# Taps in two halves, and the last feed-forwards' bias, relu, cast and residual on another engine

## The chip, the cores and the metric

One core of a Trainium2 chip runs the whole program. Its engines each work through their own list of instructions in order and wait for each other by semaphores: TensorE (PE) multiplies matrices into PSUM, VectorE (DVE) and ScalarE (ACT) work element by element on SBUF and PSUM, GpSimd (POOL) element by element on SBUF, and SyncE (SP) issues the transfers. The metric is the device time of one execution, in microseconds (us).

## The reference

Two layers of a small vision network on an input of 2 x 96 x 96 x 96 (batch, channels, rows, columns). Layer 0 adds a state-space block with a selective scan, layer 1 a block of attention over cells of 2 x 2 pixels together with a 5 x 5 depthwise convolution of the values. After either, a feed-forward of 96 - 384 - 96 is added to each pixel's channels:

```python
EXP_MUL, MAN_MUL = (5, 2)
EXP_ACC, MAN_ACC = (5, 10)
q_mul = lambda x: _float_quantize(x, EXP_MUL, MAN_MUL)
q_acc = lambda x: _float_quantize(x, EXP_ACC, MAN_ACC)

def _qlinear(x, W, b):
    y = q_acc(jnp.einsum('bsk,nk->bsn', q_mul(x), q_mul(W)))
    return q_acc(y + q_mul(b))
h = jax.nn.relu(_qlinear(x, W1, b1))
y = _qlinear(h, W2, b2)
...
t = t + _L1_ffn_ref(_ln_t(t), L1_ffn_W1, L1_ffn_b1, L1_ffn_W2, L1_ffn_b2)
```

Products are of 8-bit floats, sums are rounded to 16-bit floats, and so is the sum with the bias. In layer 1 the convolution, and what the feed-forward is given, are

```python
lepe = lax.conv_general_dilated(v.reshape(B, C, H, W), lepe_w, (1, 1), [(pad, pad), (pad, pad)], dimension_numbers=('NCHW', 'OIHW', 'NCHW'), feature_group_count=C)
...
out = out + lepe
out = jnp.einsum('oc,bchw->bohw', proj_w, out) + proj_b[None, :, None, None]
```

## The kernel before

Channels lie on the partitions. Layer 0 goes through 32 stripes (2 batches of 16), each of 6 rows or 576 pixels. For each stripe there is a front, a scan, and a back (`_l0_back`, L936), which projects, runs the feed-forward and stores x2 to device memory at L1015. Layer 1 then takes one batch after the other: `_l1_before` (L1240) loads x2 by stripes (nxt, L1253) and norms and projects them (L1258 to L1273), the attention follows, and at last `_l1_rows` (L1657) goes through 8 strips q = 0 to 7 of R = 12 rows.

A strip of `_l1_rows` projects the values into vch with an edge of two pixels (L1694, L1697), computes the near attention ft (L1719 to L1747), and adds up 21 of the 25 taps of the convolution on VectorE into acc (L1755 to L1765): one multiplication (L1759, 0.9 in the plan) and 20 fused multiply-adds (L1762, 1.43 in the plan), each over all 12 rows, 1152 columns. The other four taps, `ON_PE`, are products on TensorE (L1778). Then `project` (L1767) is called for each half c2 of 6 rows. For each quarter it forms pp on TensorE: four taps from vch (L1778), ft (L1782), and acc (L1788). VectorE adds bias and residual to make x3 (L1791). After both quarters of a half, `_plan_ffn` follows, and the half is stored (L1799).

`_plan_ffn` (L868) works on 576 pixels. The norm goes through TensorE (fxc L879), ScalarE's square (fsq L884), TensorE (fva L890), ScalarE's logarithm and exponential (L862, L863: frs or, in layer 0, in place), and VectorE's product with a cast to 8 bits (fxq L894). The hidden layer has NM = 3 blocks of 128 units. For each, TensorE forms fph (L906) for both quarters, ScalarE casts them to 16 bits (fh16, L909), adds the bias and takes the relu in place (L913), and casts to 8 bits (fh8, L916). TensorE forms fpy from the three blocks (L924), ScalarE casts it (fy16, L927) and adds the bias in place (L931), and GpSimd adds the residual x1 and gives x2 (L932).

The order of work is not that of the code. Each helper only records operations with an engine, a cost and the tiles that they read and write. `_Plan.order` (L153) then plays them through: of the operations whose operands and buffers are ready it takes for each engine the one that can start first, and among equals the one that is due first. The due times come from `_dues` (L848), which spreads the operations of a strip, as they were recorded, over a span of time (for strip q from 40 q to 40 q + 80). The instructions are issued in this order, and `_in_order` (L57) ties each engine to it. So what an engine does next is fixed at build time, and an instruction that waits holds all that stand behind it on its engine. A key beside a tile, such as (h16, m), limits a dependency to that part of the tile.

Buffers of one stage are given to the next, which waits for what last used the memory: the first loads of `_l1_before` follow the last store of the stage before, and GpSimd's memsets between the layers (L1976, L1983, L1916, L1925) and VectorE's copies (L1979, L1981) follow layer 0's last feed-forward.

Of the kernel before, what the change touches and what calls it, by code (L numbers as in the profile page):

```python
# [14 lines left out]
ALU = mybir.AluOpType  # L15
# [12 lines left out]
HW = 96  # L28
NTOK = HW * HW
WIN = 6  # L30
NW = HW // WIN
SEQ = WIN * WIN
T = WIN * HW
# [13 lines left out]
CELLS = HW // 2  # L47
# [61 lines left out]
class _Plan:  # L109
# [19 lines left out]
    def op(self, eng, cost, run, r=(), w=(), due=0.0, tab=None, also=(), scan=False, first=False):  # L129
        o = _Op(eng, cost * self.rate.get(eng, 1.0), run, due, tab)  # L130
        o.scan, o.first = scan, first
        ref = lambda t: t if isinstance(t, tuple) else (t, None)
        meets = lambda a, b: a is None or b is None or a == b
        for t, key in map(ref, r):
            o.deps.update(p for p, q in t.writes if meets(key, q))
        for t, key in map(ref, w):
            o.deps.update(p for p, q in t.writes + t.reads if meets(key, q))
        for t, key in map(ref, r):
            t.reads.append((o, key))
        for t, key in map(ref, w):  # L140
            t.writes.append((o, key))
        o.deps.discard(o)
        for t in [x[0] for x in map(ref, list(r) + list(w))] + list(also):
            if t not in o.tiles:
                o.tiles.append(t)
        for t in o.tiles:
            if not t.users and t.tag != "p":
                t.queue.append(t)
            t.users.append(o)
        self.ops.append(o)  # L150
        return o
# [713 lines left out]
    op("act", H2, run, (), (v,) if out is None else (v, out), tab="e", times=2)  # L865


def _plan_ffn(k, S, op, ps, temp, pool, bufs, ffn, x1, roomy=False):  # L868


    nc = k.nc
    cols = lambda c: slice(c * H2, (c + 1) * H2)
    xc = None if roomy else temp("fxc")
    s1, xq = temp("fsq"), S.tile(pool, [C, T], "fxq", bufs, F8)
    for c in range(2):
        def norm(c=c):
            pc, va = ps("fxc"), ps("fva")
            rs = S.tile(pool, [C, H2], "frs", 4) if roomy else None
            op("pe", H2, lambda: nc.tensor.matmul(  # L879
                pc.ap[:C, :H2], k.less_mean, x1.ap[:, cols(c)], start=True, stop=True),  # L880
                (x1,), (pc,), () if roomy else (xc,))

            def centred():
                nc.scalar.activation(s1.ap[:, cols(c)], pc.ap[:C, :H2], AF.Square)  # L884
                if not roomy:
                    nc.scalar.copy(xc.ap[:, cols(c)], pc.ap[:C, :H2])

            op("act", H2, centred, (pc,), ((s1, c),) if roomy else ((xc, c), (s1, c)),
               times=1 if roomy else 2)
            op("pe", H2, lambda: nc.tensor.matmul(  # L890
                va.ap[:C, :H2], k.mean96, s1.ap[:, cols(c)], start=True, stop=True),
                ((s1, c),), (va,), (xq,))
            _power(k, op, va, k.eps5, rs)
            op("dve", H2, lambda: nc.vector.tensor_tensor(  # L894
                xq.ap[:, cols(c)], pc.ap[:C, :H2] if roomy else xc.ap[:, cols(c)],
                rs.ap if roomy else va.ap[:C, :H2], ALU.mult, saturate=False),
                (pc, rs) if roomy else ((xc, c), va), ((xq, c),))

        norm()
    h16 = S.tile(pool, [128, NM, T], "fh16", bufs, HP)  # L900
    h8 = S.tile(pool, [128, NM, T], "fh8", bufs, F8)
    for m in range(NM):
        for c in range(2):
            def hidden(m=m, c=c):
                ph = ps("fph")
                op("pe", H2 // 2, lambda: nc.tensor.matmul(  # L906
                    ph.ap[:, :H2], ffn.w1[:, m * 128 : (m + 1) * 128], xq.ap[:, cols(c)],
                    start=True, stop=True), ((xq, c),), (ph,), (h16,))
                op("act", H2, lambda: nc.scalar.copy(h16.ap[:, m, cols(c)], ph.ap[:, :H2]),  # L909
                   (ph,), ((h16, m),))  # L910

            hidden()
        op("act", T, lambda m=m: nc.scalar.activation(  # L913
            h16.ap[:, m, :], h16.ap[:, m, :], AF.Relu, bias=ffn.b1[:, m : m + 1]),
            (), ((h16, m),))
        op("act", T, lambda m=m: nc.scalar.activation(  # L916
            h8.ap[:, m], h16.ap[:, m], AF.Copy, saturate=False), ((h16, m),), ((h8, m),))
    y16, x2 = S.tile(pool, [C, T], "fy16", bufs, HP), temp("x2")
    for c in range(2):
        def last(c=c):  # L920
            py = ps("fpy")

            for m in range(NM):
                op("pe", H2 // 2, lambda m=m: nc.tensor.matmul(  # L924
                    py.ap[:C, :H2], ffn.w2[:, m, :], h8.ap[:, m, cols(c)],
                    start=(m == 0), stop=(m == NM - 1)), (h8,), (py,), (y16,))
            op("act", H2, lambda: nc.scalar.copy(y16.ap[:, cols(c)], py.ap[:C, :H2]),  # L927
               (py,), ((y16, c),))

        last()  # L930
    op("act", T, lambda: nc.scalar.activation(y16.ap, y16.ap, AF.Identity, bias=ffn.b2), (), (y16,))  # L931
    op("pool", T, lambda: nc.gpsimd.tensor_tensor(x2.ap, x1.ap, y16.ap, ALU.add), (x1, y16), (x2,))  # L932
    return x2


def _l0_back(k, P, S, f, ffn, res, dst, at):  # L936

    nc = k.nc
    n0 = len(S.ops)
    Y, zs = f.Y, f.zs  # L940
    temp = lambda name: S.tile(P.back, [C, T], "b", 3, name=name, skip=2)
# [69 lines left out]
    for c in range(2):  # L1011
        project(c)

    x2 = _plan_ffn(k, S, op, ps, temp, P.back, 1, ffn, x1)
    S.op("sp", 1.2, lambda: nc.sync.dma_start(dst, x2.ap), (x2,), ())  # L1015
    _dues(S, n0, at)

# [151 lines left out]
def _layer0(k, tc, a, x, x2d):  # L1169


    nc = k.nc
    with ExitStack() as st:
# [34 lines left out]
        def back(n):  # L1208
            b, s = stripes[n]
            t0, t1 = (64 * n + 68) * tau, (64 * n + 135) * tau  # L1210
            _l0_back(k, P, S, F[n], ffn, x[b, :, s * WIN : (s + 1) * WIN, :],
                     x2d[b, :, s * T : (s + 1) * T], lambda v: t0 + v * (t1 - t0))

        P.wa, P.wb = S.held(k.w_ca, "w_ca"), S.held(k.w_cb, "w_cb")
        c1, split = a["off1"], 128 - C
# [441 lines left out]
def _l1_rows(k, P, S, W, ffn, M, distT, x2, out, q, at):  # L1657
# [94 lines left out]


    acc = S.tile(P.wk, [C, R, HW], "acc", 2)
    for n, t in enumerate(t for t in range(25) if t not in ON_PE):  # L1755
        def tap(n=n, t=t):
            src = lambda: vch.ap[:, t // 5 : t // 5 + R, t % 5 : t % 5 + HW]
            if n == 0:
                S.op("dve", 0.9, lambda: nc.vector.tensor_scalar(  # L1759
                    acc.ap, src(), W.lw[:, t : t + 1], None, ALU.mult), (vch,), (acc,))  # L1760
            else:
                S.op("dve", 1.43, lambda: nc.vector.scalar_tensor_tensor(  # L1762
                    acc.ap, src(), W.lw[:, t : t + 1], acc.ap, ALU.mult, ALU.add), (vch,), (acc,))

        tap()  # L1765

    def project(c2):  # L1767
        xr, x3 = S.tile(P.wk, [C, T], "xr", 2), temp("x3")
        S.op("sp", 1.0, lambda: nc.sync.dma_start(
            xr.ap, x2[:, (2 * q + c2) * T : (2 * q + c2 + 1) * T]), (), (xr,))  # L1770

        def part(c):
            pp = ps("pp")
            r0, cols = c2 * WIN + 3 * c, slice(c * H2, (c + 1) * H2)

            def some():
                for n, t in enumerate(ON_PE):
                    nc.tensor.matmul(  # L1778
                        pp.ap[:C, :H2], W.pt[:, n],
                        vch.ap[:, r0 + t // 5 : r0 + t // 5 + 3, t % 5 : t % 5 + HW],  # L1780
                        start=(n == 0), stop=False)
                nc.tensor.matmul(  # L1782
                    pp.ap[:C, :H2], W.p,
                    ft.ap.rearrange("p i n -> p (i n)")[:, (2 * c2 + c) * H2 : (2 * c2 + c + 1) * H2],
                    start=False, stop=False)

            op("pe", (len(ON_PE) + 1) * H2, some, (vch, ft), (pp,))
            op("pe", H2, lambda: nc.tensor.matmul(  # L1788
                pp.ap[:C, :H2], W.p, acc.ap[:, r0 : r0 + 3, :], start=False, stop=True),
                (acc,), (pp,), (x3,))  # L1790
            op("dve", H2, lambda: nc.vector.scalar_tensor_tensor(  # L1791
                x3.ap[:, cols], pp.ap[:C, :H2], W.pb, xr.ap[:, cols], ALU.add, ALU.add),
                (pp, xr), ((x3, c),))

        for c in range(2):
            part(c)
        y = _plan_ffn(k, S, op, ps, temp, P.wk, 3, ffn, x3, True)
        row = q * R + c2 * WIN
        S.op("sp", 1.0, lambda: nc.sync.dma_start(  # L1799
            out[:, row : row + WIN, :].rearrange("c r w -> c (r w)"), y.ap), (y,), ())  # L1800

    for c2 in range(2):
        project(c2)
    _dues(S, n0, at)

# [241 lines left out]
```

## Time and profile before

| | |
|---|---|
| three runs | 8144.84, 8158.97, 8159.37 us; median 8158.97 |
| profiled execution | 8149.47 us; from first to last instruction 8147.7 us |
| busy | VectorE 7575.8 us (93%), TensorE 7250.8 (89%), ScalarE 6328.2 (78%), GpSimd 5305.7 (65%) |
| mean granted TensorE clock | 0.963 |
| layer 0's last bias, residual, and the first product of layer 1 (start) | 6128.94, 6129.79, 6136.23 us |
| last taps, last residual of batch 0 (start) | 7097.00, 7139.15 us |
| first product of batch 1 in layer 1 (start) | 7146.01 us |
| last taps, last residual of batch 1 (start) | 8101.10, 8143.26 us |

The profile is of one execution. Times are from the first instruction on; a row names the line of the kernel, the engine, the operation and the tiles (output, arrow, inputs), the shape as partitions x columns, and how often. "Idle before" is the time that the engine did nothing ahead of a row, and the arrow names the instruction whose end let it go on. VectorE is the busiest engine over the whole, most of it in layer 0's scans and the attention's sums.

### The profile page before, as it was taken

What the parts mean: (1) busy time and instruction counts of PE and PEld (TensorE: products, weight loads), DVE (VectorE), ACT (ScalarE), POOL (GpSimd) and SP (SyncE); (2) the same over time, 40 slices, a digit from 0 to 9 for tenths busy, and PEclk for the clock granted to TensorE, in tenths of its full rate; (3) what the DMA queues carried; (4) which work ended last, traced back from release to release, by engine and by line L of the source; (5) the groups of instructions that cost most, each with busy time, mean ns of one, the idle gap of its engine ahead of it and who ended that gap; (6) DMA issues with size and microseconds to landing.
All of it is one profiled execution on the core that took longest, in us unless ns stands there. A gap on an engine that the chain in (4) does not pass through costs nothing. (4 is left out here: it accounts for less than half of the span.)

```text
span 8147.7 us, 123836 instructions
## 1 busy us (share of the span) xinstructions
PE 7250.8 (89%) x46031; PEld 3210.3 (39%) x46031; DVE 7575.8 (93%) x5276; ACT 6328.2 (78%) x10672; POOL 5305.7 (65%) x3963
## 2 busy tenths in 40 slices
PE   7888888988888888898888888888878999989998
PEld 3333344444444334343443443343334224532245
DVE  3999999999999999999999999999996998869988
ACT  5788888788788887788887878887747886778867
POOL 4888888888888888888888888888861000110001
PEclk8999999999999999999999999999998999999999
DMA  3545555444545555455445554555431000110001
GB/s 94 165 157 162 159 162 162 154 155 158 163 159 161 160 160 159 155 159 160 153 155 164 160 161 157 161 162 157 154 108 47 3 2 22 32 46 3 3 23 33
DMA packets 359852, 992.23 MB, mean 122 GB/s; under 512 B 69288, under 2 KB 71680, under 8 KB 359040
## 3 DMA queue, kind: packets, MB, share of 16 engines
q1 hardware_dynamic: 357440, 984.04, 38.5%
q8 instruction: 365, 5.98, 0.3%
q14 instruction: 255, 2.09, 0.1%
q10 hardware_dynamic: 1792, 0.12, 0.0%
HBM read 797.19 MB, written 139.25 MB: 115 GB/s over the span
## 5 line engine op out<-in xcount | busy, mean ns | idle before, releaser
L1136 POOL TENSOR_TENSOR h<-h,cre 128x864 f32<-128x864 f32 x2048 | 3481.2, 1714 | 753.5 <-DVE h L1131 507.5
L1131 DVE TENSOR_TENSOR_SCAN h<-dA,bp 128x864 f32<-128x864 f32 x2048 | 3900.0, 1939 | 61.4 <-PE y L1149 39.9
L1094 ACT ACTIVATE dA<-dlr,A 128x576 f32<-128x576 f32 x3072 | 2158.7, 766 | 830.9 <-DVE h L1131 725.4
L1114 DVE TENSOR_TENSOR bp<-dur,bp 128x864 f32<-128x864 f32 x2048 | 2075.4, 1046 | 188.4 <-DMA dur<-du_d 117.3
L1149 PE MATMUL y<-h,fold 128*32 128x288 f32 (+2 forms) x18432 | 1790.0, 434 | 221.7 <-POOL h L1136 198.7
L1509 ACT ACTIVATE pr<-sc 128x960 f32<-128x960 f32 (+1 forms) x1080 | 954.1, 937 | 203.9 <-PE sc L1505 183.4
L1149 PEld LDWEIGHTS y<-h,fold 128*32 128x32 f32 x18432 | 725.9, 113 | 974.9 <-POOL h L1136 669.5
L1110 PE MATMUL bp<-bt,selb 128*128 128x288 bf16 x2048 | 613.5, 300 | 458.7 <-DVE h L1131 440.4
L1589 DVE TENSOR_TENSOR sums<-sums,pr 128x3840 f32<-128x3840 f32 (+1 forms) x240 | 959.1, 3996 | 57.0 <-ACT pr L1509 34.5
L1681 POOL MEMSET vch<- 96x32 f32 x16 | 2.4, 154 | 1321.8 <-DVE dist L1543 1211.3
L1110 PEld LDWEIGHTS <-selb 128*128 128x128 bf16 x2048 | 197.3, 96 | 1163.0 <-DVE h L1131 956.4
L1505 PE MATMUL sc<-qH,kH 32*128 32x480 f32 (+1 forms) x3240 | 627.3, 602 | 12.6 <-issue 8.0
L1505 PE MATMUL sc<-q,kH 32*128 32x480 f32 (+1 forms) x1080 | 564.8, 602 | 0.0
L1194 PE MATMUL y<-selb,minus 128*32 128x288 bf16 x3146 | 552.0, 301 | 0.0
L1571 PE MATMUL av<-pr,vT 128*32 128x480 f32 (+1 forms) x4320 | 534.1, 565 | 3.7 <-ACT av L1596 3.5
L1762 DVE SCALAR_TENSOR_TENSOR acc<-vch,lepe_w,acc 96x1152 f32<-96x1152 f32 x320 | 467.7, 1462 | 8.4 <-ACT vch L1697 0.4
L1505 PEld LDWEIGHTS sc<-qH,kH 32*128 32x128 f32 x3240 | 219.8, 184 | 422.0 <-issue 223.7
L617 PE MATMUL pc<-xin,w_ca 128*128 128x288 f32 x1152 | 366.5, 424 | 0.4 <-DVE fxq L894 0.4
L1194 PEld LDWEIGHTS <-minus 128*32 128x32 bf16 x3146 | 274.0, 100 | 212.5 <-issue 122.3
L932 POOL TENSOR_TENSOR x<-x,fy 96x576 f32<-96x576 f32 x32 | 53.2, 1662 | 461.1 <-ACT fy L931 387.7
L791 PE MATMUL pt<-xd,w_dt 96*128 96x288 f32 x768 | 264.2, 440 | 7.7 <-ACT r L797 4.8
L810 POOL TENSOR_TENSOR e<-e,du 128x576 f32<-128x576 f32 x192 | 231.5, 1206 | 31.0 <-ACT du L806 31.0
(284 smaller groups left out, 10983.1 us busy)
## 6 DMA issues: line engine op xcount, KB each, us to landing
cre<-c_d SPq DMA_DIRECT2D x1024, 288.0 KB, 3.3
dur<-du_d SPq DMA_DIRECT2D x256, 864.0 KB, 5.2
dlr<-dl_d SPq DMA_DIRECT2D x256, 864.0 KB, 5.8
x<-xs SPq DMA_DIRECT2D x512, 72.0 KB, 2.6
du_d<-du SPq DMA_DIRECT2D x128, 288.0 KB, 3.1
dl_d<-dl SPq DMA_DIRECT2D x128, 288.0 KB, 3.7
du_d<-du SPq DMA_DIRECT2D x128, 144.0 KB, 2.5
dl_d<-dl SPq DMA_DIRECT2D x128, 144.0 KB, 2.4
```

The costliest lines, as they stand in the source:

```text
L1094: nc.scalar.activation(dA.ap[:, :, blk, :], dlr.ap[:, blk, :].rearrange("p (c n) -> p c n", c=2), AF.Exp, scale=k.A[:, i, kg, h, blk : blk ...
L1110: nc.tensor.matmul(bp.ap[:, :H2], k.selb[:, kk, i, :], f.bc[o].ap[:, toks], start=True, stop=True)
L1114: nc.vector.tensor_tensor(bp.ap[:, : NBL * H2].rearrange("p (b n) -> p b n", b=NBL)[:, ::-1], dur.ap[:, ::-1, toks], bp.ap[:, :H2].unsquee ...
L1131: nc.vector.tensor_tensor_scan(hv, dv, bv, 0.0, ALU.mult, ALU.add)
L1136: nc.gpsimd.tensor_tensor(ht.ap, ht.ap, cre.ap[:, toks].unsqueeze(1).to_broadcast([128, NBL, H2]), ALU.mult)
L1149: nc.tensor.matmul(dst, k.fold, v, start=start, stop=stop)
L1194: nc.tensor.matmul(P.awake.ap[NBL * CB :, T - HEAD + 2 * 72 : HEAD], k.minus[:, :CB], k.selb[:, 0].rearrange("p i m -> p (i m)")[:, : HEAD ...
L1505: nc.tensor.matmul(two[to // 2][:, to % 2, :n], kH[rows, k0 : k0 + 128], q, start=True, stop=True)
L1509: nc.scalar.activation(pr[:, 2 * i : 2 * i + 2, :n], two[i][:, :, :n], AF.Exp, scale=HD**-0.5)
L1571: nc.tensor.matmul((main if s < HEADS else other)[s * HD : (s + 1) * HD, :n], vT[:, blk, hd, :], pr[:, place(s, p), :n], start=at == 0, st ...
L1589: nc.vector.tensor_tensor(both, both, pr[:, :, :, :n], ALU.add)
L1762: S.op("dve", 1.43, lambda: nc.vector.scalar_tensor_tensor(acc.ap, src(), W.lw[:, t : t + 1], acc.ap, ALU.mult, ALU.add), (vch,), (acc,))
```

## The change

In the last strip of a batch (q = 7) the taps are recorded in two halves of 6 rows, 576 columns each: those of the first half before `project(0)`, those of the second before `project(1)`. Their planned cost is 0.45 for the multiplication and 0.2 + 0.615 for a multiply-add. The product of a half depends on its half of acc alone. Five feed-forwards are "last": both halves of q = 7 in either batch, and that of layer 0's last stripe. In these, bias and relu of the hidden layer, its cast to 8 bits, the output's bias, and the residual are VectorE's; the casts from PSUM stay on ScalarE. Everything else is as before. In the built program TensorE, ScalarE, VectorE and GpSimd differ in order only at these three places, and SyncE not at all.

```diff
-def _plan_ffn(k, S, op, ps, temp, pool, bufs, ffn, x1, roomy=False):
+def _plan_ffn(k, S, op, ps, temp, pool, bufs, ffn, x1, roomy=False, last=False):
...
+        if last:
+            op("dve", T, lambda m=m: nc.vector.tensor_scalar(
+                h16.ap[:, m, :], h16.ap[:, m, :], ffn.b1[:, m : m + 1], 0.0, ALU.add, ALU.max),
+                (), ((h16, m),))
+            op("dve", T, lambda m=m: nc.vector.tensor_copy(
+                h8.ap[:, m], h16.ap[:, m], saturate=False), ((h16, m),), ((h8, m),))
+            continue
         op("act", T, lambda m=m: nc.scalar.activation(
             h16.ap[:, m, :], h16.ap[:, m, :], AF.Relu, bias=ffn.b1[:, m : m + 1]),
             (), ((h16, m),))
...
+    final = last
...
+    if final:
+        op("dve", T, lambda: nc.vector.tensor_scalar(y16.ap, y16.ap, ffn.b2, None, ALU.add), (), (y16,))
+        op("dve", T, lambda: nc.vector.tensor_tensor(x2.ap, x1.ap, y16.ap, ALU.add), (x1, y16), (x2,))
+        return x2
     op("act", T, lambda: nc.scalar.activation(y16.ap, y16.ap, AF.Identity, bias=ffn.b2), (), (y16,))
     op("pool", T, lambda: nc.gpsimd.tensor_tensor(x2.ap, x1.ap, y16.ap, ALU.add), (x1, y16), (x2,))
...
-    for n, t in enumerate(t for t in range(25) if t not in ON_PE):
-        def tap(n=n, t=t):
-            src = lambda: vch.ap[:, t // 5 : t // 5 + R, t % 5 : t % 5 + HW]
...
+    parts = 2 if q == CELLS // WIN - 1 else 1
+    R1 = R // parts
+
+    def tap(n, t, p):
+        src = lambda: vch.ap[:, R1 * p + t // 5 : R1 * p + t // 5 + R1, t % 5 : t % 5 + HW]
+        dst = lambda: acc.ap[:, R1 * p : R1 * p + R1]
+        key = (acc, p) if parts > 1 else acc
+        if n == 0:
+            S.op("dve", 0.9 / parts, lambda: nc.vector.tensor_scalar(
+                dst(), src(), W.lw[:, t : t + 1], None, ALU.mult), (vch,), (key,))
+        else:
+            S.op("dve", 0.2 + 1.23 / parts, lambda: nc.vector.scalar_tensor_tensor(
+                dst(), src(), W.lw[:, t : t + 1], dst(), ALU.mult, ALU.add), (vch,), (key,))
...
-                (acc,), (pp,), (x3,))
+                ((acc, c2) if parts > 1 else acc,), (pp,), (x3,))
...
-        y = _plan_ffn(k, S, op, ps, temp, P.wk, 3, ffn, x3, True)
+        y = _plan_ffn(k, S, op, ps, temp, P.wk, 3, ffn, x3, True, parts > 1)
...
     for c2 in range(2):
+        if c2 < parts:
+            for n, t in enumerate(taps):
+                tap(n, t, c2)
         project(c2)
```

In layer 0 the last stripe's `_l0_back` is called with `last` set (`n == len(stripes) - 1`), and passes it on.

More of the change, by code (lines that the diff above doesn't have):

```diff
@@ L933, in _plan_ffn, with _l0_back @@
     return x2
-def _l0_back(k, P, S, f, ffn, res, dst, at):
+def _l0_back(k, P, S, f, ffn, res, dst, last, at):
     nc = k.nc
@@ L1012, in _l0_back @@
         project(c)
-    x2 = _plan_ffn(k, S, op, ps, temp, P.back, 1, ffn, x1)
+    x2 = _plan_ffn(k, S, op, ps, temp, P.back, 1, ffn, x1, last=last)
     S.op("sp", 1.2, lambda: nc.sync.dma_start(dst, x2.ap), (x2,), ())
@@ L1211, in back @@
             _l0_back(k, P, S, F[n], ffn, x[b, :, s * WIN : (s + 1) * WIN, :],
-                     x2d[b, :, s * T : (s + 1) * T], lambda v: t0 + v * (t1 - t0))
+                     x2d[b, :, s * T : (s + 1) * T], n == len(stripes) - 1, lambda v: t0 + v * (t1 - t0))
         P.wa, P.wb = S.held(k.w_ca, "w_ca"), S.held(k.w_cb, "w_cb")
@@ L1754, in _l1_rows @@
     acc = S.tile(P.wk, [C, R, HW], "acc", 2)
-    for n, t in enumerate(t for t in range(25) if t not in ON_PE):
-        def tap(n=n, t=t):
-            src = lambda: vch.ap[:, t // 5 : t // 5 + R, t % 5 : t % 5 + HW]
[L1758 to L1765, printed above, removed]
+    parts = 2 if q == CELLS // WIN - 1 else 1
[10 more added lines that the diff above has]
+                dst(), src(), W.lw[:, t : t + 1], dst(), ALU.mult, ALU.add), (vch,), (key,))
+    taps = [t for t in range(25) if t not in ON_PE]
     def project(c2):
```

## The prediction

> **What bounds the kernel where it is changed.** The page's busy row (VectorE 93%, ScalarE 78%) is an average over stages; the change touches three short places: the end of layer 0, and the end of layer 1 for batch 0 and for batch 1. So I read the busy table of two stretches of batch 1's end, then the timeline of each engine there. Columns of the table: stretch, length, busy us and instructions of TensorE, weight loads, VectorE, ScalarE, GpSimd, then clock and DMA.
>
> ```profile
> 8073.70:8108.30 34.60, 33.42 (x142) 20.72 (x141) 34.11 (x33) 24.80 (x55) 3.34 (x2) 1.00 0.09 26
> 8108.30:8147.70 39.40, 20.27 (x77) 11.45 (x74) 4.70 (x11) 30.48 (x64) 5.08 (x4) 0.64 0.08 23
> ```
>
> While the last taps run (first row) VectorE is full. Then it is nearly empty for 39.4 us, with ScalarE busy for 30.5. VectorE's and ScalarE's timelines say why (start, duration, instruction, idle time before it and who ended it):
>
> ```profile
> 8101.10 7.21 DVE L1762 SCALAR_TENSOR_TENSOR acc<-vch,lepe_w,acc 96x1152 f32<-96x1152 f32 x5
> 8109.63 0.52 DVE L1791 SCALAR_TENSOR_TENSOR x<-pp,proj_b,xr 96x288 f32<-96x288 f32 x1 [1.32 <-PE pp L1788]
> ...
> 8121.82 0.45 DVE L894 TENSOR_TENSOR fxq<-fxc,frs 96x288 fp8e5<-96x288 f32 x1 [5.90 <-ACT frs L863]
> ...
> 8132.24 0.45 DVE L894 TENSOR_TENSOR fxq<-fxc,frs 96x288 fp8e5<-96x288 f32 x1 [9.16 <-ACT frs L863]
> ```
>
> ```profile
> 8114.55 1.00 ACT L909 CAST fh<-fph 128x288 f16<-128x288 f32 x3 [0.20 <-PE fph L906]
> 8115.59 0.78 ACT L913 ACTIVATE fh<-fh,f1b1g 128x576 f16<-128x576 f16 x1
> 8116.39 0.68 ACT L916 ACTIVATE fh<-fh 128x576 fp8e5<-128x576 f16 x1
> ...
> 8140.03 0.68 ACT L916 ACTIVATE fh<-fh 128x576 fp8e5<-128x576 f16 x1
> ...
> 8142.35 0.77 ACT L931 ACTIVATE fy<-fy,f1b2g 96x576 f16<-96x576 f16 x1
> ```
>
> Three feed-forwards remain after the taps: the second half of q=6 (6b) and both halves of q=7 (7a, 7b); 6a, the first half of q=6, is just being finished. ScalarE takes them in turn without a gap: hidden layers 8114.6 to 8121.0, 8124.8 to 8131.3, 8134.3 to 8140.7. VectorE waits for it 5.9 and 9.2 us. What follows the last bias:
>
> ```profile
> 8143.26 1.27 POOL L932 TENSOR_TENSOR x<-x,fy 96x576 f32<-96x576 f32 x1 [7.46 <-ACT fy L931]
> 7140.45 0.32 SPq L1799 DMA_DIRECT2D out<-x  x1
> 7142.90 5.64 SPq L1253 DMA_DIRECT2D nxt<-x2d  x4
> 7146.01 4.12 PE L1258 MATMUL nxc<-nxt,less_mean 96*96 96x288 f32 x8 [8.22 <-DMA nxt<-x2d]
> ```
>
> The first line ends batch 1: x2 is complete at 8144.53, and the rest to 8147.7 is its store. The others are batch 0's end, the same picture 1004.1 us earlier: the store of x2, then the load of batch 1, then TensorE, idle 8.2 us for it. So what x2 gains is passed on whole. At layer 0's end too: bias until 6129.71, GpSimd's residual until 6131.08, store, load at 6133.38, TensorE at 6136.23 after 7.75 us of idling.
>
> **Prices.** From the list of groups by shape (line, instruction, count, busy us, mean ns):
>
> ```profile
> L1762 DVE SCALAR_TENSOR_TENSOR acc<-vch,lepe_w,acc 96x1152 f32<-96x1152 f32 x320 | 467.7, 1462 | 8.4 <-ACT vch L1697 0.4
> L1759 DVE TENSOR_SCALAR acc<-vch,lepe_w 96x1152 f32<-96x1152 f32 x16 | 13.0, 809 | 16.0 <-DMA xn<-xd 8.2 <-ACT vch L1697 7.8
> L1592 DVE TENSOR_TENSOR sums<-sums 128x960 f32<-128x960 f32 x8 | 9.3, 1158 | 0.3
> L284 DVE CAST f1w1q<-f1w 96x384 fp8e5<-96x384 f32 x1 | 0.4, 356 | 0.6 <-DMA f1b<-in_b 0.6
> L1981 DVE COPY join<-ident 32x32 f32<-32x32 f32 x1 | 4.4, 4447 | 0.0
> ```
>
> - *Half tap.* The adds of 3840 and 3072 columns (4.156 and 3.356 us) give 1.04 ns a column. Five taps in a row take 7.21 us, a step of 1.445; so the fixed part is 1.445 - 1.20 = 0.245, and a half (576 columns) costs 0.845. A rule speaks against halving: the Trainium skill, "VectorE: DVE Perf Modes", section on the TRN2 errata, says that the latency of SBUF is paid per instruction, so many small tiles pay it many times; its formula, N + 151 cycles at 0.96 GHz, is a fixed part of 0.157. By the rule 21 added instructions cost 3.3 us a batch, by the row 5.1. The row counts also the wait of each tap for the one before it, so I take the row.
> - *Fp8 cast* of 576: the cast row and the copies (960 in 0.653, 3840 in 2.155: 0.52 ns a column) give 0.356 + 192 x 0.52 = 0.46.
> - *Bias and relu* on 16-bit data: no row of VectorE has 16-bit input. The nearest is L1759: 0.809 for 1152 fp32 columns, 0.6 plus 0.21 fixed. At that rate 576 cost 0.51. The same page, perf-mode tier table, has tensor_scalar at twice that rate on 16-bit data: an estimate of 0.15 + 0.21 = 0.36. I take 0.36; with 0.51 the final sum is 3 us smaller; at one column per 1.04 ns it would be 0.81.
> - *Residual* (two SBUF inputs, 576): 1.158 - 384 x 1.04 ns = 0.76, against 1.27 on GpSimd.
>
> **Layer 0's end.** ScalarE's six casts stay; the first three end at 6121.87 as before, the rest by 6122.8. Relu and cast of one block of 128 on VectorE are 0.36 + 0.46 = 0.82 with the step between; three blocks from 6121.93 end at 6124.4, where ScalarE ended at 6127.30. From there to the second y16 cast was 1.61 us (6127.30 to 6128.91); it stays: 6126.0. Bias 0.06 + 0.36, residual 0.03 + 0.76: 6127.2 instead of 6131.08. **Gain 3.9 us.** GpSimd's memsets of 4.7 us, queued behind the removed residual, now start after VectorE's bias, beside VectorE's residual. The rule against this ("SBUF — State Buffer", who interferes with whom: a VectorE instruction in a two-port mode, or with two SBUF inputs against a GpSimd reader, waits for the whole GpSimd instruction) is borne out by L1981: 4.447 us for 32 columns, until the memsets ended. Memsets do not read, so I charge the residual nothing; blocked, it would end 4.6 later and the gain would be -0.7. The copies behind it wait, but have until the first xn at about 6139.
>
> **A batch's end (twice).** Times are batch 1's.
> 1. *Taps.* Before: 34.6 us from 8073.69 to 8108.3. Added: 21 x 0.245 = 5.1, and the two adds of x3 for 7a (0.43 each), which now come before the last seven half taps. End 8108.3 + 5.1 + 0.9, less 0.1 for some changes of instruction and stretches by GpSimd: 8114.1. Queued behind them on VectorE: fxq of 6b. Its rs is ready at 8111.5 (8111.4 before; the fpy of 6a starts 0.2 later on TensorE), so it is 2.6 us late; this is what halving costs.
> 2. *What halving buys.* In TensorE's new order the last products of 7a (L1788 in the old numbers) stand before the fpy of 6a. They need the first half's taps: 8073.69 + 0.61 + 20 x 0.845, and 2.6 for the other VectorE instructions among them, is 8093.8. TensorE reaches them at 8102.0, behind the products that fill it, and waits for nothing. x3 of 7a is done at 8107.2 (8111.0 before), and its norm goes ahead of 6b's hidden layer.
> 3. *6b* stays on ScalarE: fxq 8114.1 to 8114.55, first cast 8114.9; the second, behind a product of 7b on TensorE, ends at 8115.85; then 3 x 0.81 + 2 x 0.59 + 0.68 + 2 x 0.61: last fp8 cast 8121.35 (8121.0 before).
> 4. *7a.* ScalarE then does one rs (0.79), four casts of 7a (1.3), 6b's y16 and bias (0.66 + 0.7) and a square (0.3): 3.75, so its first block is ready for VectorE at 8125.1. There 6b's residual, still on GpSimd, runs from 8124.55 to 8125.8; by the rule and row above the relu waits for it: 8125.85. Three blocks of 0.82: 8128.3 (ScalarE before: 8131.3). Second y16 cast 1.61 later: 8129.9; bias and residual: 8131.15.
> 5. *7b.* fxq at 8129.1, the first two casts after 7a's y16 casts: 8130.55; VectorE is free from the residual at 8131.2. Three blocks: 8133.65. y16: 8135.25. Bias 0.42, wait and residual 0.86: 8136.5. Before: 8144.53. **Gain 8.0 us.**
>
> ScalarE loses 14 of its instructions here (2 x 4.9 us by their steps of 0.81, 0.59 and 0.7); 8.0 of the 9.8 arrive, since VectorE starts later and its work stands in the chain.
>
> **Sum.** 2 x 8.0 + 3.9 = 19.9 us against the profiled execution's 8149.47: 8129.6. Against the median shown, 8158.97, it is 8139. The runs lie at 8145 and at 8159, and I can't tell from which a new median comes: the middle, **8134**.
>
> **Rivals.**
> - *16-bit runs at one column per 1.04 ns.* Relu 0.81, cast 0.75: 2.3 us more a feed-forward and 0.45 a bias. Gains 2.5 a batch, 1.1 at layer 0: 6 in all, 8148. For it: no 16-bit row. Against: the fp32 rows already run at twice that. Chance 0.1.
> - *The next stage takes nothing*, because another wait ends there: only batch 1's 8.0 remain, 8146. Against: both next stages' loads follow the store. Chance 0.1.
> - *TensorE's queue*: each late product of 7a holds fpy and 6b behind it, and ScalarE starts 6b some 2 us later in both batches: gain 16, 8138, inside the range. Chance 0.12.
> - *Slower: half taps cost nearly a whole tap.* If 576 columns cost 1.445, the taps end 24 us later, and all behind them: 16 slower a batch, 28 in all, 8182 on the same base. It decides from 0.845 + 8.0 / 40 = 1.05 us a half. Against: 960 columns take 1.158. Chance 0.05.
>
> **Numbers.** The forecast holds 0.63. Range 8116 to 8151: a gain of up to 25 (0.1 less a half tap) on the faster runs, of 8 on the slower. Runs of this kernel can't tell less than 0.2% (16 us) from none. My own 20 clears that narrowly: most of the forecast's chance counts as faster, the first three rivals mostly as the same. Faster 0.58, same 0.37, slower 0.05.
>
> **What would show it.** Half taps at a step of 0.85 and ending near 8114; relu near 0.36 and cast near 0.46; VectorE idle before relu only for ScalarE's casts; from the last taps to the last x2 some 22 us instead of 36; batch 1's first load about 12 us earlier (3.9 + 8.0). Wrong, if relu shows 0.8, if a relu or residual stretches to the length of a GpSimd instruction, or if the load moves by less than x2 does.

## The result, and the profile after

| | before | after |
|---|---|---|
| median of 9 runs each, us | 8158.39 (8144.84 to 8165.44) | 8139.08 (8121.35 to 8150.58) |
| ratio, with 95% interval | | 0.9974 (0.9964 to 0.9984) |
| profiled execution, first to last instruction, us | 8147.7 | 8125.7 |

The kernel after is faster by 0.16% to 0.36%: the ratio makes it about 21 us, the two medians 19.3. The two profiled executions differ by 22.0 us. The two profiles, laid side by side at the places that the change touches, show where these went:

| from, to | before, us | after, us | gain, us |
|---|---|---|---|
| start, to the first fxq of layer 0's last stripe (nothing changed so far) | 6119.84 | 6116.88 | 2.96 |
| to the first product of layer 1 (layer 0's end) | 16.39 | 12.88 | 3.51 |
| to q = 7's first tap in batch 0 (nothing changed) | 933.36 | 933.15 | 0.21 |
| to the first product of batch 1 (batch 0's end) | 76.42 | 69.18 | 7.24 |
| to q = 7's first tap in batch 1 (nothing changed) | 927.68 | 927.05 | 0.63 |
| to the last x2 (batch 1's end: the *stage* below) | 70.84 | 63.45 | 7.39 |
| to the last instruction | 3.17 | 3.11 | 0.06 |

18.1 us come from the three places of the change; 3.9 us come from stretches whose instructions are the same, and belong to the two executions, not to the change.

The busy table of batch 1's end in the kernel after, cut at the end of the last taps (stretch, length, busy us and instructions of TensorE, weight loads, VectorE, ScalarE, GpSimd, then clock and DMA), answers the first one shown of before:

```profile
8059.14:8100.50 41.36, 39.96 (x168) 25.07 (x167) 40.34 (x57) 29.31 (x65) 4.75 (x3) 1.00 0.10 27
8100.50:8125.70 25.20, 14.60 (x48) 7.25 (x47) 10.58 (x25) 15.96 (x39) 1.27 (x1) 0.60 0.09 27
```

The first stretch has grown from 34.6 to 41.4 us, with VectorE still full, and the second has shrunk from 39.4 to 25.2; ScalarE's busy time in it fell from 30.5 to 16.0. VectorE's timeline there (start, duration, instruction, idle time before it and who ended it):

```profile
8093.70 6.80 DVE L1778 SCALAR_TENSOR_TENSOR acc<-vch,lepe_w,acc 96x576 f32<-96x576 f32 x7
8100.43 0.81 DVE L894 TENSOR_TENSOR fxq<-fxc,frs 96x288 fp8e5<-96x288 f32 x2
...
8108.81 0.45 DVE L894 TENSOR_TENSOR fxq<-fxc,frs 96x288 fp8e5<-96x288 f32 x1 [5.72 <-ACT frs L863]
8111.69 0.96 DVE L914 TENSOR_SCALAR fh<-fh,f1b1g 128x576 f16<-128x576 f16 x1 [2.42 <-ACT fh L909]
8112.68 0.46 DVE L917 CAST fh<-fh 128x576 fp8e5<-128x576 f16 x1
8113.05 0.36 DVE L914 TENSOR_SCALAR fh<-fh,f1b1g 128x576 f16<-128x576 f16 x1
...
8121.44 0.37 DVE L940 TENSOR_SCALAR fy<-fy,f1b2g 96x576 f16<-96x576 f16 x1 [1.64 <-ACT fy L935]
8121.84 0.75 DVE L941 TENSOR_TENSOR x<-x,fy 96x576 f32<-96x576 f32 x1
```

The first two rows are 7b's last half taps and, queued behind them, fxq of 6b. Then VectorE waits for ScalarE again (5.72 and 2.42 us). The blocks of 7a begin with a relu that takes 0.96 us where the next takes 0.36. The last x2 is complete at 8122.59. ScalarE and GpSimd in that time:

```profile
8101.24 0.40 ACT L909 CAST fh<-fph 128x288 f16<-128x288 f32 x1 [0.87 <-PE fph L906]
...
8107.31 0.68 ACT L923 ACTIVATE fh<-fh 128x576 fp8e5<-128x576 f16 x1
```

```profile
8111.20 1.27 POOL L944 TENSOR_TENSOR x<-x,fy 96x576 f32<-96x576 f32 x1 [13.87 <-ACT fy L943]
```

6b's hidden layer is on ScalarE from 8101.24 to 8107.99. GpSimd's row is 6b's residual: it runs from 8111.20 to 8112.47, beside the long relu. Batch 0's end and the next load, in the timelines of VectorE, the queue of SP and TensorE:

```profile
7125.61 0.75 DVE L941 TENSOR_TENSOR x<-x,fy 96x576 f32<-96x576 f32 x1
7128.84 1.25 SPq L1265 DMA_DIRECT2D nxt<-x2d  x3
7132.09 1.25 PE L1270 MATMUL nxc<-nxt,less_mean 96*96 96x288 f32 x2 [7.35 <-DMA nxt<-x2d]
```

x2, load and first product come 14.06, 14.06 and 13.92 us earlier than before; the next stage takes all of it but 0.14. Of the 13.92, by the table, 10.75 are the change's (3.51 and 7.24) and 3.17 come from the unchanged stretches. Layer 0's end, on VectorE and GpSimd:

```profile
6118.94 0.37 DVE L914 TENSOR_SCALAR fh<-fh,f0b1g 128x576 f16<-128x576 f16 x1 [0.81 <-ACT fh L909]
...
6123.44 0.75 DVE L941 TENSOR_TENSOR x<-xr,fy 96x576 f32<-96x576 f32 x1
6124.11 3.98 DVE L1998 COPY join<-ident 128x96 f32<-128x96 f32 x1
```

```profile
6123.73 2.19 POOL L1935 MEMSET xs<- 96x2500 f32 x1
6125.85 2.18 POOL L1944 MEMSET dist<- 96x2500 f32 x1
```

The residual of 0.75 us runs beside a memset and is not stretched; the copy behind it takes 3.98 us, until the memsets end. And the prices, from the list of groups by shape (count, busy us, mean ns):

```profile
L1778 DVE SCALAR_TENSOR_TENSOR acc<-vch,lepe_w,acc 96x576 f32<-96x576 f32 x80 | 69.7, 871 | 2.0
L917 DVE CAST fh<-fh 128x576 fp8e5<-128x576 f16 x15 | 6.9, 460 | 0.5
L914 DVE TENSOR_SCALAR fh<-fh,f0b1g 128x576 f16<-128x576 f16 x3 | 1.1, 366 | 0.8 <-ACT fh L909 0.8
L941 DVE TENSOR_TENSOR x<-x,fy 96x576 f32<-96x576 f32 x4 | 3.0, 754 | 0.1
```

### The profile page after: what moved, and what is told of

It is laid out like the page before. It is cut to its first block, busy times and chain, and to the rows that moved or that the text cites. A ratio compares the mean times of both kernels' runs of the same rounds, so it can differ in the third digit from the quotient of the medians.

```text
span 8125.7 us, 123877 instructions
## 1 busy us (share of the span) xinstructions
PE 7230.7 (89%) x46031; PEld 3201.2 (39%) x46031; DVE 7601.1 (94%) x5358; ACT 6297.2 (77%) x10637; POOL 5295.5 (65%) x3958
## 5 line engine op out<-in xcount | busy, mean ns | idle before, releaser
L1143 DVE TENSOR_TENSOR_SCAN h<-dA,bp 128x864 f32<-128x864 f32 x2048 | 3899.9, 1939 | 62.5 <-PE y L1161 40.4
L1778 DVE SCALAR_TENSOR_TENSOR acc<-vch,lepe_w,acc 96x1152 f32<-96x1152 f32 (+1 forms) x360 | 478.7, 1330 | 9.8 <-ACT vch L1709 0.8
```

What stands on the lines that cost most here:

```text
L1143: nc.vector.tensor_tensor_scan(hv, dv, bv, 0.0, ALU.mult, ALU.add)
L1778: S.op("dve", 0.2 + 1.23 / parts, lambda: nc.vector.scalar_tensor_tensor(dst(), src(), W.lw[:, t : t + 1], dst(), ALU.mult, ALU.add), (vch ...
```

## Experiments

Whole times of one kernel differ by 20 us and more from run to run, so the experiments are read from the stage: q = 7's first tap in batch 1 to the last x2. Its first part, the 40 half taps with what stands between them, took 41.35, 41.36, 41.36 and 41.37 us in the four kernels that have it unaltered. Batch 0's stage is a second reading: it is within 0.01 us of batch 1's in ten of the twelve kernels; in e8 it is 58.52 us instead of 58.64, in e11 62.05 instead of 62.37. Diffs are against the kernel after; where an edit adds lines, an experiment's line numbers are up to three above after's.

| kernel | taps end | stage | ratio to before, 95% interval |
|---|---|---|---|
| before | 34.62 | 70.84 | |
| after: halves, 7a and 7b moved | 41.36 | 63.45 | 0.9974 (0.9964 to 0.9984) |
| e1: halves alone | 41.35 | 71.32 | 1.0001 (0.9993 to 1.0009) |
| e2: feed-forwards alone | 34.62 | 62.33 | 0.9975 (0.9967 to 0.9984) |
| e3: after, 6b's bias and residual too | 41.36 | 62.56 | 0.9975 (0.9966 to 0.9984) |
| e4: after, all of 6b too | 41.37 | 57.04 | 0.9960 (0.9947 to 0.9974) |
| e5: e4 without halves | 34.61 | 56.39 | 0.9965 (0.9954 to 0.9976) |
| e6: e4, fxq of 6b before three half taps | 41.98 | 56.76 | 0.9965 (0.9952 to 0.9979) |
| e7: after, fxq of 6b before three half taps | 41.97 | 62.17 | 0.9973 (0.9964 to 0.9982) |
| e8: e5, two of TensorE's taps on VectorE | 38.35 | 58.64 | 0.9963 (0.9949 to 0.9976) |
| e9: e5, one of TensorE's taps on VectorE | 35.99 | 54.63 | 0.9958 (0.9944 to 0.9971) |
| e11: after, 6a's residual on VectorE | 41.37 | 62.37 | 0.9978 (0.9969 to 0.9986) |

### One part of the change at a time: e1 and e2

e1 keeps the halves, and no feed-forward is "last":

```diff
-        y = _plan_ffn(k, S, op, ps, temp, P.wk, 3, ffn, x3, True, parts > 1)
+        y = _plan_ffn(k, S, op, ps, temp, P.wk, 3, ffn, x3, True)
...
-                     x2d[b, :, s * T : (s + 1) * T], n == len(stripes) - 1, lambda v: t0 + v * (t1 - t0))
+                     x2d[b, :, s * T : (s + 1) * T], False, lambda v: t0 + v * (t1 - t0))
```

> Measure: the stage from q=7's first tap to the last x2 of batch 1 (70.84 us before, 63.45 after). Theory (after the taps ScalarE's queue sets the end, so halving of itself buys nothing): taps end 41 us after their start instead of 34.6, 6b's first cast comes about 1.2 later than before, and all three feed-forwards follow it on ScalarE as before: stage 72 us (70.5 to 73), layer 0's end as before, whole time 8157 to 8163. Rival (the halving brings the gain, since 7a's norm goes ahead of 6b's hidden layer): stage 67 or less, whole time 8150.

Stage 71.32 us: 0.48 longer than before, and the whole time is before's. The halves do bring 7a's x3 forward, from 37.4 to 34.6 us after the first tap, but the end doesn't gain by it. At layer 0's end the way from fxq to the next layer's first product took 16.51 us (before 16.39, after 12.88), so those 3.5 us belong to the feed-forward there.

e2 keeps the feed-forwards and makes whole taps:

```diff
-    parts = 2 if q == CELLS // WIN - 1 else 1
+    parts = 1
...
-        y = _plan_ffn(k, S, op, ps, temp, P.wk, 3, ffn, x3, True, parts > 1)
+        y = _plan_ffn(k, S, op, ps, temp, P.wk, 3, ffn, x3, True, q == CELLS // WIN - 1)
```

> Same measure. Theory: taps end 34.6 us after their start as before, 6b's hidden layer is as before, the two feed-forwards of q=7 lose 14 instructions of ScalarE: stage 64 us (63 to 65.5), so that the halves in the change are worth less than 1.5 us a batch; whole time 8140. Rival (halves are needed, because without them 7a's x3 comes after the taps and VectorE's blocks wait): stage 67 or more, whole time 8146.

Stage 62.33 us, shorter than after's by 1.12 and below the 63 to 65.5 that I expected. So the feed-forwards bring the whole gain (8.51 us by themselves), and the halves, with them, cost 1.1. Why whole taps that all end before 7a's x3 cost nothing is seen in e2's timeline of VectorE and TensorE, from the last taps on:

```profile
8082.25 7.20 DVE L1778 SCALAR_TENSOR_TENSOR acc<-vch,lepe_w,acc 96x1152 f32<-96x1152 f32 x5
...
8096.55 0.51 DVE L1807 SCALAR_TENSOR_TENSOR x<-pp,proj_b,xr 96x288 f32<-96x288 f32 x1 [0.41 <-PE pp L1804]
```

```profile
8091.49 2.11 PE L1794 MATMUL pp<-vch,pt 96*96 96x288 f32 x8
...
8095.37 0.65 PE L906 MATMUL fph<-fxq,f1w1q 96*128 96x288 fp8e5 x4
8095.86 0.65 PE L1804 MATMUL pp<-acc,proj_w 96*96 96x288 f32 x2
```

The taps end at 8089.45, but TensorE still has 7b's products with vch to do and reaches the last product with acc at 8095.86. For 7b's x3 VectorE waits for TensorE, not the reverse, so having a half of the taps sooner gives it nothing.

### GpSimd beside VectorE: e3 and e11

In e3 the output bias and the residual of 6b are VectorE's too (`last or end` in place of `last` for the closing part, `end` set for q = 6, c2 = 1).

> Same measure. Theory (7a's first relu is stretched by GpSimd's residual of 6b beside it): with 6b's output bias and residual on VectorE that relu takes 0.36 instead of 0.96 us, the three blocks of 7a end about 1 us earlier, stage 62.5 us; whole time 2 us less than after, not to be told from it by the times. Rival (the relu's length does not matter, ScalarE's casts set the end): stage 63.4.

Stage 62.56 us, 0.89 less. In e3's VectorE timeline 6b's residual stands before 7a's first relu, which now has its own length:

```profile
8140.76 0.75 DVE L941 TENSOR_TENSOR x<-x,fy 96x576 f32<-96x576 f32 x1
8141.43 0.36 DVE L914 TENSOR_SCALAR fh<-fh,f1b1g 128x576 f16<-128x576 f16 x1
```

So the stretch of 0.6 us was GpSimd's residual. The edit also takes a bias of 0.77 us from ScalarE. The traces divide the gain: counted from the first tap, the relu starts at 52.24 us instead of 52.55, 0.31 earlier, and is 0.60 shorter.

e11 asks the same of the half taps. In the kernel after three of them in a row take 3.42 us, of which two steps of 0.845 and a length of 0.81 make 2.50; GpSimd's residual of 6a runs beside them (VectorE's row, then GpSimd's):

```profile
8095.39 3.42 DVE L1778 SCALAR_TENSOR_TENSOR acc<-vch,lepe_w,acc 96x576 f32<-96x576 f32 x3
```

```profile
8095.94 1.39 POOL L944 TENSOR_TENSOR x<-x,fy 96x576 f32<-96x576 f32 x1 [16.13 <-ACT fy L943]
```

```diff
-    op("pool", T, lambda: nc.gpsimd.tensor_tensor(x2.ap, x1.ap, y16.ap, ALU.add), (x1, y16), (x2,))
+    eng, on = ("dve", nc.vector) if end else ("pool", nc.gpsimd)
+    op(eng, T, lambda: on.tensor_tensor(x2.ap, x1.ap, y16.ap, ALU.add), (x1, y16), (x2,))
...
-        y = _plan_ffn(k, S, op, ps, temp, P.wk, 3, ffn, x3, True, parts > 1)
+        y = _plan_ffn(k, S, op, ps, temp, P.wk, 3, ffn, x3, True, parts > 1, q == CELLS // WIN - 2 and c2 == 0)
```

> Measure: from q=7's first tap to the end of its last half tap (after 41.36 us, predicted 40.4). Edit: in the kernel after, 6a's residual is VectorE's and not GpSimd's; the planner then also puts the first half of 6b's fxq before the last half tap. Theory (the missing 0.9 us is a half tap that GpSimd's residual of 6a stretches): 0.9 less for the stretch, 0.7 more for the residual, 0.4 more for fxq, so the taps end at 41.5 and no half tap is long in the last seven. Rival (GpSimd's residual takes nothing from VectorE): 42.4. Stage 63.3 us by the theory, 64 by the rival.

Taps end at 41.37 us, with the residual and one fxq more in front of the end, and e11's VectorE row shows six half taps without a long one, (5.05 - 0.81) / 5 = 0.85 a step:

```profile
8109.45 5.05 DVE L1779 SCALAR_TENSOR_TENSOR acc<-vch,lepe_w,acc 96x576 f32<-96x576 f32 x6
8114.43 0.75 DVE L945 TENSOR_TENSOR x<-x,fy 96x576 f32<-96x576 f32 x1
```

The theory holds for the taps. The stage, 62.37 us, is 0.9 shorter than I expected. Two things differ there: the first half of fxq, now before the last half tap, lets ScalarE's first cast of 6b come at 41.14 us instead of 42.10, and 6b's residual now runs after 7a's first relu (8126.65 against 8123.96), which takes 0.37. What each is worth was not separated.

### What halving costs: e7

fxq of 6b is put before the last three half taps, by letting these depend on it:

```diff
+    S.fxq = xq
...
+    behind = [S.fxq] if parts > 1 else []
...
-                dst(), src(), W.lw[:, t : t + 1], dst(), ALU.mult, ALU.add), (vch,), (key,))
+                dst(), src(), W.lw[:, t : t + 1], dst(), ALU.mult, ALU.add),
+                [vch] + (behind if p and n > 17 else []), (key,))
```

> Same measure, against after (63.45). Edit: the same move of fxq in the kernel after. Theory (the cost of halving is that fxq of 6b stands behind the half taps, and ScalarE's queue passes it on to the end): first cast of 6b 2.3 us earlier, stage 61.4 us (61 to 62), less than e2's 62.33. Rival (the cost of halving is elsewhere, in the later last taps themselves): stage 63.4 to 64.3.

Stage 62.17 us, 1.28 less, although the taps end 0.6 later. The first cast of 6b came only 0.96 earlier, not 2.3; e7's VectorE and TensorE show who held it:

```profile
8086.77 0.81 DVE L895 TENSOR_TENSOR fxq<-fxc,frs 96x288 fp8e5<-96x288 f32 x2
...
8099.29 0.96 DVE L915 TENSOR_SCALAR fh<-fh,f1b1g 128x576 f16<-128x576 f16 x1 [2.42 <-ACT fh L910]
```

```profile
8085.25 2.11 PE L1797 MATMUL pp<-vch,pt 96*96 96x288 f32 x8
...
8088.16 0.53 PE L907 MATMUL fph<-fxq,f1w1q 96*128 96x288 fp8e5 x3
```

fxq is there at 8087.58, but TensorE, in its fixed order, is still at products of 7b and of 7a's norm and comes to fph at 8088.16; and ScalarE's order has the logarithm and frs of 7a (8088.36 to 8089.27) before the cast, which starts at 8089.17.

The gain is larger than the 1.12 us that the halves cost, and that cost is not the lateness of fxq alone. From the end of 7a's first relu to the last x2 it is 9.94 to 9.96 us in after, e2, e3 and e7, so the difference can be read at that relu. e2's residual of 6b on GpSimd, and the relu:

```profile
8105.55 1.27 POOL L944 TENSOR_TENSOR x<-x,fy 96x576 f32<-96x576 f32 x1 [13.20 <-ACT fy L943]
8106.84 0.37 DVE L914 TENSOR_SCALAR fh<-fh,f1b1g 128x576 f16<-128x576 f16 x1 [2.62 <-ACT fh L909]
```

Without halves the residual has ended (8106.82) when the relu starts. In after the relu starts 0.54 us later, counted from the first tap, and takes 0.59 longer, since the residual falls on it. The first part is of the size of e1's 0.48, where no relu is VectorE's. e7 takes away lateness alone: its relu starts 1.29 earlier than after's and still takes 0.96.

### More of the same: e4, e5 and e6

e4 makes 6b a "last" feed-forward as well:

```diff
-        y = _plan_ffn(k, S, op, ps, temp, P.wk, 3, ffn, x3, True, parts > 1)
+        y = _plan_ffn(k, S, op, ps, temp, P.wk, 3, ffn, x3, True, parts > 1 or (q == CELLS // WIN - 2 and c2 == 1))
```

> Same measure. Theory (ScalarE is still what the end waits for): 6b's bias, relu, 8-bit cast, output bias and residual on VectorE take 5.1 us from ScalarE, and VectorE has 8 us of idling there: stage 58.5 us (57.5 to 60), last taps to last x2 17 us instead of 22.1; whole time about 8129. Rival (VectorE's list in order becomes the bound, or TensorE's): stage 61 or more, whole time 8135 or more.

57.04 us: 6.4 less than after, more than the 5.1 us taken from ScalarE and below the 57.5 to 60 that I expected. The long relu goes too; the rest of the difference was not followed up. e5 is e4 without halves (`parts = 1`, and the last three feed-forwards of a batch "last").

> Measure: the stage from q=7's first tap to the last x2 of batch 1 (before 70.84 us, after 63.45, e2 62.33, e4 57.04). Theory (halving costs a batch's end about 1.1 us, as e2 against after shows, and goes on costing it when ScalarE is relieved of 6b too): stage 56 us (55.3 to 56.8), whole time a few us under e4's. Rival (with ScalarE relieved, 7a's early norm is what counts, so the halves pay at last): stage 57.5 or more.

56.39 us: the halves cost 0.65 here. e6 is e4 with e7's edit.

> Same measure, against e4 (57.04). Edit: 6b's 8-bit product fxq is put before the last three half taps instead of behind them. Theory (6b's lateness behind the taps is on the path): 6b's first cast 2.3 us earlier, taps end 0.8 later, stage 55.5 us (54.8 to 56.5). Rival (7b's own chain from the last taps sets the end): 0.8 later, stage 57.8.

56.76 us, between the two: 0.28 won where I expected 1.5. The planner put 6b's blocks, which wait for ScalarE's casts, before x3 of 7b in VectorE's order, so that this x3 is done 45.9 us after the first tap instead of 43.9. That this is why so little was won was not tested:

```profile
8116.69 0.46 DVE L918 CAST fh<-fh 128x576 fp8e5<-128x576 f16 x1
8117.06 0.45 DVE L895 TENSOR_TENSOR fxq<-fxc,frs 96x288 fp8e5<-96x288 f32 x1
8117.43 0.93 DVE L1810 SCALAR_TENSOR_TENSOR x<-pp,proj_b,xr 96x288 f32<-96x288 f32 x2
```

### The other way round: e8 and e9

If TensorE is what holds the end of a batch, as e2 shows, VectorE should get more taps, not smaller ones. e8 is e5 with two of TensorE's four taps on VectorE in q = 7:

```diff
+    on_pe = ON_PE if q < CELLS // WIN - 1 else ON_PE[:2]
-    taps = [t for t in range(25) if t not in ON_PE]
+    taps = [t for t in range(25) if t not in on_pe]
...
-                for n, t in enumerate(ON_PE):
+                for n, t in enumerate(on_pe):
...
-            op("pe", (len(ON_PE) + 1) * H2, some, (vch, ft), (pp,))
+            op("pe", (len(on_pe) + 1) * H2, some, (vch, ft), (pp,))
```

> Same measure, against e5. Edit: in q=7 two of the four taps that TensorE forms go to VectorE, no halves. Theory (without halves TensorE's queue, full until 41 us after the first tap, holds 6b's first product and 7b's last products, while VectorE has ended at 34.6): taps end at 37.5, TensorE has 3.9 us less, x3 of 7b is done about 2.5 us earlier, stage 2.5 us less than e5's (53.5 us if that is 56). Rival (ScalarE sets the end): e5's stage within 0.6 us.

58.64 us, 2.25 longer than e5: I was wrong in sign. e8's VectorE and TensorE:

```profile
8086.55 11.00 DVE L1778 SCALAR_TENSOR_TENSOR acc<-vch,lepe_w,acc 96x1152 f32<-96x1152 f32 x7
8097.48 0.81 DVE L894 TENSOR_TENSOR fxq<-fxc,frs 96x288 fp8e5<-96x288 f32 x2
```

```profile
8097.61 3.19 PE L1805 MATMUL pp<-acc,proj_w 96*96 96x288 f32 x6 [3.68 <-DVE acc L1778]
```

TensorE has done all else and waits 3.68 us for acc: the bound has passed to VectorE, and fxq of 6b stands behind the taps again. Seven taps take 11.00 us instead of 6 x 1.445 + 1.41 = 10.1; so about 0.9 us are lost among them, with a GpSimd residual beside them from 8093.91 on. With one tap (`ON_PE[:3]`) the two should meet:

> Measure: the stage from q=7's first tap to the last x2 of batch 1 (e5 56.39 us, e8 58.64). Edit: as e8, but one of TensorE's four taps goes to VectorE instead of two. Theory (VectorE's taps and TensorE's queue meet at 7b's last products, and two taps put VectorE past TensorE: in e8 fxq of 6b stood behind taps that ended at 38.4 us): taps end at 36.9, TensorE has 1.95 us less and is not made to wait, x3 of 7b some 1.5 us earlier than e5's, stage 54.7 us (54 to 55.5). Rival (e5 stands at the balance already, any tap moved costs): 56.4 or more.

54.63 us. e9's last rows on VectorE:

```profile
8071.62 8.65 DVE L1778 SCALAR_TENSOR_TENSOR acc<-vch,lepe_w,acc 96x1152 f32<-96x1152 f32 x6
...
8084.29 0.51 DVE L1808 SCALAR_TENSOR_TENSOR x<-pp,proj_b,xr 96x288 f32<-96x288 f32 x1 [0.56 <-PE pp L1805]
```

The taps end at 8080.27 and 7b's x3 is done at 8084.80, 40.5 us after the first tap, 1.7 earlier than in e5. This version has the shortest stage: 8.8 us a batch below after and 16.2 below before. Its whole time, 8116.15 us by the median of 5 runs, is 0.42% below before's (0.29% to 0.56%). By whole times alone the intervals of e9 and after overlap; that e9 is the faster of the two rests on the stage.

## Why the prediction was right

8134 us were predicted and 8139.08 measured, a gain of 19.9 against 19.3 by the medians and about 21 by the ratio. That this fits so closely is in part luck: of the profiled difference of 22.0 only 18.1 are the change's, so the terms were a little too large, and the rest came from unchanged stretches. The 5 us between 8134 and 8139.08 are the choice of a base halfway between two runs; from the median shown the same sum gives 8139.

- *What bounds it.* ScalarE's queue after the taps: right. e1, e2 and e4 show it: no ScalarE work removed, no gain; 6b's work removed too, 6.4 more. The moved steps are also shorter on VectorE (relu and 8-bit cast 0.36 and 0.46 us, on ScalarE 0.78 and 0.68); no run separates the shorter steps from the relief of the queue.
- *Prices.* Half tap 0.845 (0.85 in undisturbed rows, 871 ns mean with the stretched ones), cast 0.46 (0.460), relu 0.36 (0.366), residual 0.76 (0.754). The estimate of twice the fp32 rate for relu on 16-bit data held, and with it the first rival, one column per 1.04 ns, falls; the slower rival, half taps near a whole one, falls too.
- *Layer 0's end.* fxq to the last x2: 11.24 us before, 7.31 after, a gain of 3.9 as predicted. The memsets took nothing from the residual, as assumed. But only 3.5 reached the next layer's first product: from x2 to it the load took 5.57 us instead of 5.15. The prediction had it passed on whole.
- *Batch's end, step 1 (taps).* This is the mis-sized term. Predicted 40.4 us after the first tap (its terms, added up, make 40.5), measured 41.36. The sum took 0.1 off "for some changes of instruction and stretches by GpSimd". With the taps longer, 6a's residual on GpSimd, which before ran after them (from 8109.93), now falls on them and stretches one by 0.9 (e11). The rule that the prediction used elsewhere (the Trainium skill, "SBUF — State Buffer", who interferes with whom: a VectorE instruction with two inputs in SBUF contends with a GpSimd instruction that reads it) covers a tap as well, and I had not applied it there.
- *Step 2 (what halving buys).* 7a's x3 does come before the taps end, and the first half of its norm goes ahead of 6b (frs at 8099.97). But the second half waits on ScalarE until 6b is through (8107.90). The prediction listed a cost and a benefit of halving and never set one against the other. The runs do: the cost is larger, by 0.5 us alone (e1) and by 1.1 together with the feed-forwards (e2). About half of the 1.1 is the later start of 7a's relu, with fxq late as e7 shows; the other half is the relu's stretch, which e2 doesn't have. The forecast stayed right since it summed the whole.
- *Steps 3 to 5.* Moved to before's clock (14.55 us), 6b's first cast comes at 8115.8 (predicted 8114.9), x2 of 7a at 8132.0 (8131.15), of 7b at 8137.1 (8136.5): the 0.9 of step 1 is carried on, and partly made good. The relu blocked by 6b's residual was predicted in step 4 and is there (e3), though the list of signs counts a stretched relu as a sign of being wrong. Gain 7.39 instead of 8.0, and 7.24 up to batch 1's first product at batch 0's end.
- *The range.* Its lower end, 8116, does not come out of its own terms (8145 less 25 is 8120); the measured time lies far from it.
- *Rivals.* "The next stage takes nothing" falls: 10.75 us of the change reached batch 1's first product. TensorE's queue did hold fph of 6b in e7, but not the 2 us per batch of that rival. 7a's second x3 came 1.1 us later than reckoned for another reason: its product with acc was through at 8091.41 on TensorE, and x3, which stands behind three half taps in VectorE's order, started at 8093.27.

## What to carry to other kernels

When work is drained from a full queue at the end of a stage, ask first which engine each later step waits for: here taking instructions from ScalarE paid almost one for one, while splitting VectorE's work into halves brought forward an x3 that the end did not wait for, and pushed back an fxq that it did wait for. Making one engine's work longer can drag another engine's instruction into its time, as with GpSimd's residual on the taps and on the relu: list what runs beside the old end as well as in it. Where whole times scatter more than the effect, compare a stage between two fixed instructions across kernels, and move a balance by the smallest unit (one tap won 1.8 us, two lost 2.3).

## What the runs showed of the hardware

- Layer 0's instructions up to its last feed-forward are the same in all these kernels, yet the first fxq of that feed-forward started anywhere from 6113.55 us (e2, mean granted clock of the execution 0.966) to 6148.66 us (e3, clock 0.957). That spread of 35 us is larger than the whole effect of the change; on the whole the executions with the lower mean clock were the later ones. Up to that fxq TensorE was busy for 5334.2 us in e2 and 5385.5 in e3, VectorE for 5837.7 and 5839.7. The stages of a batch's end repeated within 0.01 us from batch 0 to batch 1, but for e8 (0.12) and e11 (0.32).
- A VectorE addition with two inputs in SBUF (0.75 us) was not stretched by the GpSimd memsets beside it, while a copy behind it took 3.98 us (0.21 before), until the same memsets ended. A multiply-add lost 0.9 us and a relu 0.6 to a GpSimd addition beside them (e11, e3).
